# A new order of the pieces of a hand-scheduled transformer block, with equal tile modes of TensorE side by side

## The chip, the core and the metric

The kernel runs on one core of a Trainium2 chip. A core has five engines with a queue each: PE (TensorE, the matrix engine, whose weight loads are shown apart as PEld), DVE (VectorE), ACT (ScalarE), POOL (GpSimd) and SP (SyncE, which here only issues DMAs). Each engine works through its own instructions in order and waits on semaphores for the others. The metric is the device time of one execution in microseconds (us). Before the change the median of three runs was 3693.19 us (3692.50 to 3694.23).

## The reference

The computation is one block of a transformer with adaptive layer norm, for 8 sequences of 512 tokens with 128 features each.

```python
h = layernorm(x) * (1 + ca) + sa
x = x + ga * attention(h)          # 16 heads of 64, causal over all 512 tokens, softmax
h = layernorm(x) * (1 + cb) + sb
x = x + gb * local_layers(h)       # six layers, see below

for i in range(6):                 # local_layers
    x = attn_layer(shift_tokens(x), ...) + x
    x = ffn_layer(shift_tokens(x), ...) + x
```

`attn_layer` makes q, k and v of 16 heads, divides q and k by their norms, scales and rotates them by position, and lets each window of 32 tokens attend to itself and to the window before it. `ffn_layer` is a layer norm, a product to 2 x 341 features, one half times the GELU of the other, and a product back to 128. `shift_tokens` takes the second half of the features from the token before. All is float32.

## The kernel before

The work has two parts. The first is the global attention, in which the weights of the local layers are prepared beside it. The second is the six local layers. Each part is a set of software pipelines. A stage is a Python generator that emits a small piece of work, on one engine as a rule, and yields. `streams_of` gives each stage a letter and chains its pieces over all items in order. `run` then walks through a string of letters and emits the next piece of the stage that each letter names:

```python
with tc.manual_schedule():
    for s in order:
        next(streams[s])
```

So the string is the order in which every engine's queue is filled. `ORDER1` (5442 letters) is the string of the first part and `ORDER` (15688 letters) that of the second. Nothing reorders instructions later, and semaphores are set where a buffer or a value asks for one.

In the second part an item is a tile of 128 tokens. There are 4 tiles in a sequence, 8 sequences and 6 layers, so 192 tiles, and every stage below runs once for each tile (the number of pieces is in brackets):

- PE: `c` project (4: q and k, a 128x512 product in three matmuls each, lines L380 to L382), `j` turn_qk (4: four 128x128 transposes each, L937), `l` score (2, L981), `r` values (4: 128x512 products), `v` turn_p (2: four transposes each, L1080), `x` combine (2, L1106).
- ACT: `a` operand, `d` square (4, L856), `k` keep_qk (4: two pieces copy the turned keys into kbd by two half copies each, L946; two copy the turned queries, L950), `z` mask (2, L958), `o` exps (2, L1014), `s` keep_values (4, L1053), `w` keep_p (2, L1089), `y` keep_y (L1121).
- DVE: `e` rotate (4, L865), `g` square_sum (4, L892), `m` top (2, L995), `n` less_top (2, L1002), `p` denominator (4, L1022 and L1025). `h` inverse goes over DVE, ACT and POOL for two tiles at a time.
- POOL: `b` operand_rest, `f` rotate_sum (4, L883), `i` scale (2, L925), `q` divide (2, L1033).
- SP: `t` store (4, L1062) and `u` fetch (4, L1068), which write the values to DRAM and read them back in another layout for combine.

The letters `F` to `N` are the feed-forward layer of a sequence, with `F` its PE pieces (transposes L375, products, and L1149), `G` its ACT pieces (L1167 among them), `H` POOL and `I` DVE.

A matmul uses the PE array in a tile mode, given by how many rows and columns of the array it takes. Products and transposes use all of it, 128*128. Scores and combine work window by window, on 32 columns each, so they run in the mode 128*32, four windows side by side. In the first part the mixing of the values (L649) runs in 128*64 and the folding of weights (L745) on 64 rows.

The buffers that tie the stages together are few. PSUM has four banks for products, in turn (`psum_mm`: project, values, combine and the feed-forward layer share them), two for transposes (`psum_tr`) and one for each of the two halves of the scores (`sp0`, `sp1`). A PE piece that writes a bank waits until the engine that empties it is done.

```python
turn = {"mm": itertools.cycle(range(4)), "tr": itertools.cycle(range(2))}
```

In the first part the scores have two PSUM banks (`ss0`, `ss1`), products and transposes two each.

Of the kernel before, what the change touches and what calls it, by code (L numbers as in the profile page):

```python
# [27 lines left out]
    "aabaabcbcdcecefzargsfdecbedfrgfesdgcfgdcettbrcezdfsrgtfesdagcfgdrecscgdfettrbcesfduhucfehhhtgfedhhrgfrgsdhdgri"  # L28
    "sgtcasrdijejkcgcfdjkecbikejslkgdlfmdgjfejkrinckmrerzfajuuttuutsnjschfkghklethhzhsmlhobndfdmrzghocinscpzrdgiojp"
    "ptdjerkqekcfjpgsrkgjqaoelkftuuuutspldmfvppvwmcqwpncdqgzuxtesuidxnvyveocfwrgwtogfjsjekxipxkhcufdppujhyhhtcezqkj"  # L30
    "rpekqdlsglhmdfvnvhmwfrzgtruwnhscbgaiocezxoestfxdpjdfujygkrppickgcersqpjttedjkqrkgldufuagslmstfvnvwmcbzubncwieo"
    "rzxeofdxtspdfujgyFkppqcIrditjseckcefjtjkphrqkgrhuesufhhvdvgwtrsgfFadlIhhlIwbmhIcinmxzestrInxdfIuuojycoigkctptj"
    "serkjippckjezqlkpdguqlsumdgftvndvwrmfzeFsriGncwgrGeuajfotjsxgdfkhcHgckejtbxhkehhutslfyoFFdmdhpfGuppuhpGjrqnFFg"
    "GqgtcsIkvhidrwevsrawgbczfjzeltsikxmdxnfuugoFtjIjitykcrekicosjpdrefkuruzsrppftdjgslpaqglkmqFnmbvzvIuwcwntcsueoj"
    "zjefdrkcgftFFestdkhgfhFohhdprhIrhshriastjppckgcqdpcedqjjestlfglkfmxeikxmvnduvuygwfrznFwgbcsIojxkeFlIItutuioizd"
    "xfpuucyIjmdIrppqIkrstlasbpnrqmzveFwGvunfcGgzceHwctseujofxdkgxfedrtygoftcsgjpjddhrppkqreuhckuhhpajgsqFFtkeshGhG"
    "gvfvcflewldhmfwtFFgdniGmczuuIFdnijteorrIfsjgscgkbcerkjtiecdfjktgrdfkejarssgilohdxtsfzxphmhlhkupphuqrnyFpsmhqzF"
    "FIuuttnbhgoFizvIvowciwjejkcpfrkejdcsppdfckterqrseajfjpglgfdtlsmdgqxknxbmzgjkuicnutryuekiuoFtvsIlwfcmveFwrIIduf"
    "jduxsnkxoIgIpyIczrzdlstppqaFmjGpbnrqukejrGgjfkcgtchHesvhkchfvhuewdjwtglstfeoxkhmohxfdpdFFnuyzhuippGltpGgFFmqnG"
    "rqgzuoIvijcrwescstvfderwFagsfucdIkrebticstgojjedrkfcpdFppfkjsIjqktrpezcqasgjledflkmtfnxmzixgkFFnuuygdbohgjutho"  # L40
    "FhhukpvhIvhzwhriwcspprtdpqcesjdjqgkcevfdrwgrfseltsiaglkmxnfmxzntvbyuocuwFeorxsIfdjcpkjgrekFslIIuuttiizdxIfmcyp"
    "pjIdprnuqIkrzulsqsteaFbvmGfcnwvuGejwcHkgrefjdtjscgkfugrekjdlkhgtfhsxmhhtzxnohhdhlzigyuFFomupGtppGicjeFFkqpncGq"
    "IdujejzfckgFfekrdvsIfvwgtcwujidelogximxkndlogfzcpymrdpprqseartsbjtspjnfkFgcIqkjeFFukuofdtvgvowpFwhpprhqhhcIsrd"
    "hjhpsehrtqakcgsfuurzecbrdfetsvtvwgicdcwerfgjdjagdlfselkitmxmkxnfgjzuncusbtiyjkeuroukFslfIxmFnjIIozidlztktpxImr"
    "IyppcsqIrdrpesuqFuacGnfvtsevGcbwgrHweuojdjfckgxgfketsxudhlofghyphhFFdzmhhGpppGthrqtcnqgjrezivsFFukudGgfvtwlIus"
    "iwrmcnsajdbckertjdgfjseFkcIfukreoctitjgleskxfzmdxndfglzugyuoirtmcpsjndrkppqceFsajdpfIjoeFFktqgkvfvuugzwhFwbhro"
    "IthhrshchtsphcidpprdejrqkpescaqjgjstcgfdlgdfelkxmitekxvnfyuvumwrzgfjuuwncstbkFteiorzlIsfxmFnxIIodizjycpkrIgdIl"
    "uppuqIsrtcpseqaFdjmGufrekcbvnGfvwectsHjwecokjfugrgkfjedtlstkgfxzmdxhdnhloguhhzupryhmhFFthsppiGpGunFFgqrIGjqsjk"
    "ritcsvkecrwefajdvsgFftudtwcgkbxIoieljzmfjonckpixzdelkuuppjfrmdpjqynstckgrqecksgvfdvewFawFFbgdfIuozhFoghcphhrIh"
    "hdjhckeldtisppluqmxpefxnqjymjzrgfknckgiceFtsrtoefvdrwIrdfacsgubjuevkctsgFwfcejlIIuodzfdkplIppImqIpnFqstmuGveix"  # L50
    "zGvnwxgwHogtjtdjfocgykrpixesukxhufppjhdtcpuhhkgjqdrykerqszcgshFFfeaGrhGfvvbdlhwtgisuFFmwnGliIzjmFkncIocejjerfd"
    "cogdfceztFstkefFFkIfgjupFkupplqtddIuxxmlgynrgzrmscpsntiiquajdvoberwckgfretscstvhoefjdchwgfrhjuhkexusphhkfxtppd"
    "udlgqzgjymFhkrpnqrIzvsltisuawvmbFwinrIIrostjtIocIkrpIxadbxppsuqjuyejkctpgfrsekjrqkdcfuzgvdvwcewtiFsuleGfGlgdmH"
    "cmstjtndfcgkxnizexduoFFeuyfoGtprfpprGugjqjpsgFFsqhaGrbkItFscIhreckjfhhuezrtstvklfwdldmhhgvhsuinruwmcztgscuiand"
    "jdrekjbcefkjrgfkcetsujoirezklogdlfpdtmxstfppxnqcypmzrgqsujnuavdgbckitersvewFfwFFogdIfuogzFpstjhpphqjhhukcIrkhj"
    "hdphcqktetsxdiglelfmxmvnfyFutgzurIiwrsvsnFacwIIubocdIjoIerdkcIfxexstjyefzjukrpcfkgjeFdilktGgtlppsqdmGjpmfjkrnu"
    "rgqzuncktHgcaevsivsrewdrwgcfdhojjfuzetxhshhukgxfkolydphlbsmhtthFFppinGpGcmqrgdurznuqsejavstickgFFewfGvIdrwfgco"
    "FebtrsIjfdjuukcgicektrsteojfcdkpldfezximlsppxnqctpymzurugqejdvsfFwnaFFIktfgogbvuudFhwghocIhhzjjdhhtrkphirescst"
    "ppjkqrdgkrpeqxsagflstlfmxnimzjuynvukctbcewvoFzeuuicwfdrIdjsfrkejxsgfkFglIIttdoixpjIyppcIuurmdqIkrtslspnaqFezvb"
    "GcmfwvueGjwcHktgreufjdjsnckfgxektxtdgoflygohrzphdFFmuhhsuppGhhtpGcqnjerqFFzgfdGvgkrhIwivaslustwcuimcndjedrbkje"  # L60
    "fFsjkIcfttgrkeoicjglesfxztmkxfondpluziugdrppyrsmqjtspnrakqgcvesbcwvoefrdwjgsFfkhjFFIuuthkhhtdFohghzhpciIcdtrdi"
    "jesrkjesrafjtppscqgcpelqgldfmkxmfkexjbnyudfvugkrznvuuitwgctsFoerwiocIjrfeFalIIkzbfdjdplkImIuxppuqIsxstrypmqFnc"
    "GgvzvunGcewHcwojetfjsdgxkfuexdgkfrtgyotlhsphdFFmhhzppGhhupuGcqnreqjtFFzgfdGvgkrhIiwvasluswcimtjundckerbjdgfjse"
    "FkcIfttkreojicglesoxfkmtzxpdfnlduppyuzqrmcspnirteocsFgaqoejdvfkFFIpwfgvuutzppjbdrqwgkFphqgjhIschhktcdhvhdehvwi"
    "rwejscktfgrgdjfcsejdligtelkxfmmkxnfjgzujuniykrukuFascIobrresFsjIItitofcdlzpdIgIlmppxqIkxuucypeqtFdjGnrfkmrejGc"
    "znHvkecwfavsgjwtlgdfuesuxkbomxfdhortyzpFFhsnhhGpplhhpGtgqrmcqgzuFFnduhseiGtvovuIcgfrewcwijsejdrkgtFfrdIsfjugsc"
    "kicertktaejocfskpjdlfedzxmbflkpptxnqpmzjuygcquknriedvvoFgwwgFFfdIshogtjhuzpFhhukpprqIcshajhdtrbkpehrqsctgsfvdv"
    "wceiwrdgcsefrdtjgslfaelkimxgtnxfmzryunubFsuijIorkcjseFkxIIuttiozfldpxImIcppyqrIdjrkpueqsFulaGnftsgcGmbzujgHvdc"
    "nkerwcdgfvoetjsrwekfrjugoxfhktsxzplhypphhtdjqmFFkpnqsuguGlhthGchmivndvFFzuewiGgjwrIkfctujsejakcbfredFksgrftdtI"
    "jocgicersoeliskxptzmfxdppdlyuqnurpmzqtcgsnavdfvgwFwebjockIfreojjsprfuutktgFFppsqdhpkFgqhzchhIvhvhdwhcetiwcdgce"  # L70
    "djfjklgfedlkimxejxfnkmjuzfgrukunjysrgktiFourIscasbjeFlIIoizdflkpIxmtIppxqrItycsnrdpumzFquresGvtcnsfGvugwreHzca"
    "wgjfdcekjbretfsujkxgdfohlkoglhdpthhxtsmhppFFhyqnGpquGcmgFFuezhiGtvnvducIwwfjgdckeirjdgrsekfFtjgscfIakreobulixm"
    "sxnofzpczippyjdjdtprgtkecqslkeqcmfdvgvwFnwfFFeooIfdrprgusuppjaqjkgctuphbFehqsjhhkIkfldzvghlhmwhnvmrzwncxoestii"
    "cuofdrpdcgzppxdqstejtyjkerfrkpgfFgcuasIujqcktscbeFlefxIIuddfcmjIeItrxesfyIukfltgitFndvGgrgzivGmcshwdHnjhwcehho"
    "xukheuhfcotgjzfjupkxehkjppdflkgdplqymdgFFqnGrGmnFFzsGtigiFIuorIFFsFIabFrtIrsoctsjpdjkpprqcekjrefkjausrpguqkcst"
    "lfuzedlbmdfvmvwgrwncnzvtisveuiwxwgdxofgorhtystjphjhhkppcqcpekjqcuesujfkxdtkugfldezvhvhmwfldgwnxhmzrtigyuFnsria"
    "IorsjrkbtFtcIIsjoxdIpIkexursuIyfcatsrdppbjqejkckpglfuzelqmdtFgsufrnGcmizgcGdnrtseHvtdvwceofjwcogfkjeuxuispxtde"
    "krfppjuysrgakfjpgzlhkqdlmhstqughhFFnGhhGmrbnchzitvdtvsFFewiwgGrIojucfuretscsajfderkFgbfrdIkjugcktijesuloikpxdm"
    "zxppqstlntycpfgzmrdqnrevsujuawcbgoftvseFkcIfrdeojwFFpdfkgpptjqusFgukphzcqIhrhhdchesthjthdvikgcwevdrwfgjgrfecsa"
    "jdblstfelkimxmknxfgtjzunruykiFocsIrjesFlIIitukuotfzxdplImIppxqIcyjdpnrqkeFcGmvfzvnGruewuHcsajgwfrkejbdgjfkgcst"  # L80
    "huldehoxhhkmfoxgzpcdhnyhlhstppiudFFzgpeGGqFFmtqgtFGnrfIorIirsucausjeobctsrkeufFdpjfdjIkFFppqkgzFptgisucIcdqrde"
    "cistvevtwcwgfrgdrdgfjsejaklbestflkmxfmxngzvtnyvuwurhwujhsjuhhkchrhtekhtjiscorkeolfzpdjmfdlkppxqmpxnqgzcunyisuv"
    "eovtcwgwrfdeForspfuajdIxkbxppqstjygFkcpIIuizldgIrqettjscImrdnfIkrzliuasueFstjmfGucgkrnbveGcwHvezcdjfwgtrsgkjfu"
    "exdxhkfghdlthhsgtFFyhomhhoniGpppuuGcjrqejFFztipkdlsIGqugrkmvfncswvecatwbrzeuidjsjgkFfcIkjdfttelkolgimxmdxnfogr"
# [1237 lines left out]
```

## Time and profile before

| | |
|---|---|
| median of three runs | 3693.19 us |
| the profiled execution | 3693.09 us, its span 3691.3 us |
| PE busy | 97% of the span |
| DVE, ACT, POOL busy | 88%, 81%, 78% |
| first part (global attention) | up to about 860 us |
| second part (six local layers) | from there to the end |
| granted PE clock | 0.991 |

The profile is of one execution. "Busy" is the share of the span in which an engine has an instruction under way, so instructions that overlap in the engine's pipeline are counted once. Rows of waits name the waiting engine, its tile and line, who ended the wait, the sum in us, how often, and the longest. Rows of the timeline give the start, the length, the engine, line and operation, what it writes and reads, the tile mode (rows*columns of the array) for PE, the shape and how many like it follow each other. Matmuls are pipelined: the length of one is its way through the array, and what it costs the next is the distance of their starts.

### The profile page before, as it was taken

The page shows a single profiled execution, that of the slowest core. Times are in us where ns is not written, and L with a number is a line of the kernel's source. Part 1 is how long each engine was busy: PE and PEld are TensorE (multiplying, and loading weights), DVE is VectorE, ACT ScalarE, POOL GpSimd, SP SyncE. Part 2 cuts the span into 40 slices and gives each one's busy share as a digit, 9 for nine tenths or more (in the row PEclk, how much of TensorE's full clock was granted, in tenths as well). Part 3 has the DMA queues.
Part 4 walks back from the last instruction along what each step waited for, and adds up shares of the span by engine and source line. Part 5 has one row for each costly group of instructions (what it writes and reads, how often), then busy time and mean ns, then how long its engine had stood idle before and what let it go on. Part 6 is the DMA issues. An engine that isn't in the chain of part 4 may idle for free. (4 is left out here: it accounts for less than half of the span.)

```text
span 3691.3 us, 106123 instructions
## 1 busy us (share of the span) xinstructions
PE 3572.9 (97%) x40364; PEld 2776.9 (75%) x40364; DVE 3242.5 (88%) x6198; ACT 2977.8 (81%) x6342; POOL 2895.4 (78%) x3232
## 2 busy tenths in 40 slices
PE   7999999998999999999999999999999999999998
PEld 4566656665788878888788788888878887788786
DVE  5788988898999889999898889999898898989895
ACT  4666766676888888888888888988989888888886
POOL 3555556557998888898898888889888898888884
PEclk8999999999999999999999999999999999999999
DMA  7777778763554666546656557555666555666554
GB/s 193 199 188 191 180 193 177 179 148 101 146 145 135 164 179 166 155 134 166 179 154 163 137 158 183 155 159 137 168 179 163 150 143 147 184 161 160 154 161 110
DMA packets 352245, 594.75 MB, mean 161 GB/s; under 512 B 57198, under 2 KB 87532, under 8 KB 351740
## 3 DMA queue, kind: packets, MB, share of 16 engines
q1 hardware_dynamic: 349772, 585.70, 60.0%
q8 instruction: 323, 5.29, 0.6%
q10 hardware_dynamic: 1616, 2.16, 0.2%
q14 instruction: 182, 1.49, 0.1%
q0 software_dynamic: 352, 0.10, 0.1%
HBM read 254.52 MB, written 232.61 MB: 132 GB/s over the span
## 5 line engine op out<-in xcount | busy, mean ns | idle before, releaser
L883 POOL TENSOR_TENSOR rq<-u 128x512 f32<-128x512 f32 x768 | 983.2, 1292 | 144.9 <-DVE u L865 136.3
L865 DVE TENSOR_TENSOR u<-ps_mm,tab 128x1024 f32<-128x1024 f32 x768 | 926.3, 1218 | 127.6 <-PE ps_mm L382 63.6
L925 POOL TENSOR_TENSOR rq<-rq,rs_o 128x1024 f32<-128x1024 f32 x384 | 729.3, 1908 | 6.2
L621 POOL TENSOR_TENSOR pr<-pr,rd 128x512 f32<-128x512 f32 (+3 forms) x512 | 357.9, 721 | 297.7 <-DVE rd L614 279.2
L892 DVE TENSOR_REDUCE ss<-sq 128x8 f32<-128x512 f32 x768 | 511.5, 675 | 46.0 <-ACT sq L856 44.0
L856 ACT ACTIVATE sq<-ps_mm 128x512 f32<-128x512 f32 x768 | 458.9, 607 | 85.7 <-PE ps_mm L382 36.1
L1053 ACT COPY vh<-ps_mm 128x512 f32<-128x512 f32 x768 | 451.3, 593 | 80.7 <-PE ps_mm L382 56.9
L1033 POOL TENSOR_TENSOR pr<-pr,rd 128x256 f32<-128x256 f32 x768 | 457.1, 622 | 58.1 <-DVE rd L1025 44.5
L946 ACT COPY kbd<-ps_tr 64x512 f32<-64x512 f32 x768 | 446.3, 581 | 34.2 <-PE ps_tr L937 18.7
L937 PE MATMUL ps_tr<-ident,rq 128*128 128x128 f32 x3072 | 445.2, 274 | 4.2 <-DVE xs L1180 1.1
L937 PEld LDWEIGHTS ps_tr<-ident,rq 128*128 128x128 f32 x3072 | 363.3, 140 | 107.6 <-issue 25.9
L981 PE MATMUL sc<-kbd,qT 128*32 128x128 f32 (+1 forms) x13056 | 408.3, 266 | 7.5 <-issue 3.5
L602 ACT ACTIVATE pr<-ss,mx 128x512 f32<-128x512 f32 (+3 forms) x512 | 270.5, 529 | 176.5 <-DVE mx L592 155.9
L1106 PE MATMUL ps_mm<-v,pT 128*32 128x128 f32 x11904 | 401.8, 274 | 7.5 <-issue 7.3
L981 PEld LDWEIGHTS sc<-kbd,qT 128*32 128x32 f32 x13056 | 334.2, 109 | 69.8 <-issue 42.5
L1106 PEld LDWEIGHTS ps_mm<-v,pT 128*32 128x32 f32 x11904 | 341.4, 110 | 35.6 <-issue 24.9
L380 PE MATMUL ps_mm<-wvo,xa 128*128 128x512 f32 x768 | 347.0, 452 | 3.9 <-ACT sq L856 3.9
L380 PE MATMUL ps_mm<-wqk,xa 128*128 128x512 f32 x768 | 344.9, 449 | 5.7 <-ACT sq L856 4.0
L382 PE MATMUL ps_mm<-wqk,xa 128*128 128x512 f32 x768 | 304.8, 397 | 0.0
L382 PE MATMUL ps_mm<-wvo,xa 128*128 128x512 f32 x768 | 304.6, 397 | 0.0
L381 PE MATMUL ps_mm<-wvo,xa 128*128 128x512 f32 x768 | 303.0, 394 | 0.0
L381 PE MATMUL ps_mm<-wqk,xa 128*128 128x512 f32 x768 | 302.8, 394 | 0.0
(144 smaller groups left out, 8035.2 us busy)
## 6 DMA issues: line engine op xcount, KB each, us to landing
vd<-vh SPq DMA_DIRECT2D x768, 256.0 KB, 3.9
v<-vd SPq DMA_DIRECT2D x768, 256.0 KB, 5.1
both<-hi SPq DMA_DIRECT2D x384, 128.0 KB, 2.4
both<-lo SPq DMA_DIRECT2D x384, 128.0 KB, 2.4
wqk_d<-wqk SPq DMA_DIRECT2D x20, 512.0 KB, 3.4
wvo_d<-wvo SPq DMA_DIRECT2D x20, 512.0 KB, 3.8
wqk<-wqk_d SPq DMA_DIRECT2D x20, 512.0 KB, 4.1
wvo<-wvo_d SPq DMA_DIRECT2D x20, 512.0 KB, 4.8
```

The lines of the kernel that those rows point to most:

```text
L380: nc.tensor.matmul(ps, lhsT=xa[0], rhs=xb[0], start=start, stop=False)
L381: nc.tensor.matmul(ps, lhsT=xa[0], rhs=xb[1], start=False, stop=False)
L382: nc.tensor.matmul(ps, lhsT=xa[1], rhs=xb[0], start=False, stop=stop)
L856: nc.scalar.activation(sq, st["qk"][c], AF.Square)
L865: nc.vector.tensor_tensor(u, st["qk"][c].unsqueeze(1).to_broadcast([P, 2, 8, HD]), tabs[st["t"]][:, ts(c // 2, 2), :].unsqueeze(2).to_broa ...
L883: nc.gpsimd.tensor_tensor(r, a, b[:, :, ::-1, :], ALU.add)
L892: nc.vector.tensor_reduce(st["ss"][:, st["t"] % 2, ts(c, 8)], sq, AX.X, ALU.add)
L925: nc.gpsimd.tensor_tensor(rq, rq, rn[:, ts(side, 16)].unsqueeze(2).to_broadcast([P, 16, HD]), ALU.mult)
L937: nc.tensor.transpose(pt[:, ts(j, P)], flat[:, j, :], ident)
L981: nc.tensor.matmul(o[:, :, s], lhsT=q, rhs=kbd[:, :, j, k : k + n].rearrange("p e (s k) -> p e s k", k=WIN), start=False, stop=True, skip_ ...
L1033: nc.gpsimd.tensor_tensor(prg, prg, rd.unsqueeze(2).to_broadcast([P, 8, WIN]), ALU.mult)
L1106: nc.tensor.matmul(y[ts(w, WIN), :], lhsT=pT[:, s, g, ts(w, WIN)], rhs=vals, start=s == 1 and g == 0, stop=g == 3 and (s == 0 or (t == 0 a ...
```

## The change

Both strings are replaced. The pieces are the same, each letter appears as often as before, and the pieces of one stage keep their own order. What differs is how the stages are interleaved: pieces that use PE in the same tile mode stand next to each other more often. No function, buffer or shape changes.

```diff
 ORDER = (
-    "aabaabcbcdcecefzargsfdecbedfrgfesdgcfgdcettbrcezdfsrgtfesdagcfgdrecscgdfettrbcesfduhucfehhhtgfedhhrgfrgsdhdgri"
-    "sgtcasrdijejkcgcfdjkecbikejslkgdlfmdgjfejkrinckmrerzfajuuttuutsnjschfkghklethhzhsmlhobndfdmrzghocinscpzrdgiojp"
...
+    "aabaabcbcdcecefzargsfdecbedfrgfesdgcfgdrettbcsrgdftescargdbfescrgdfesccgdfettzrceusfudhcftehhhgfedhhrgfrgsdhdt"
+    "gcisgradceijdjgkcecfkjgbkejfslkdfelrmidmrncagfzuuttuutjesjrkinrkhfgjthsjhhzcbkhkehlshidldmsgconfojejzrikpcmkre"
...
 )
```

In the built program PE changes its tile mode 1097 times before and 857 times after: 445 and 397 times in the first part, 652 and 460 times in the second. In the second part the stretches of 128*32 work go from 326 to 230.

## The prediction

> **What bounds the kernel now.** I read the page first, then the busy time by stretch, then PE's own waits, then PE's instructions one by one.
>
> ```profile
> span 3691.3 us, 106123 instructions
> PE 3572.9 (97%) x40364; PEld 2776.9 (75%) x40364; DVE 3242.5 (88%) x6198; ACT 2977.8 (81%) x6342; POOL 2895.4 (78%) x3232
> ```
>
> The reader sees four engines that are all well used, with PE on top. By stretch (columns: PE, weight loads, DVE, ACT, POOL busy us, granted clock):
>
> ```profile
> 0.00:860.00 860.00, 795.24 (x4424) 526.50 (x4424) 712.83 (x2042) 557.22 (x1585) 458.29 (x642) 0.98 0.73 179
> 1500.00:2000.00 500.00, 497.94 (x6402) 404.27 (x6401) 452.64 (x742) 438.96 (x863) 438.76 (x472) 1.00 0.58 158
> 2000.00:2500.00 500.00, 497.60 (x6531) 404.36 (x6530) 450.63 (x747) 435.62 (x856) 438.62 (x465) 1.00 0.59 159
> 3600.00:3692.00 92.00, 75.00 (x949) 56.09 (x947) 53.78 (x102) 56.40 (x102) 41.80 (x44) 0.91 0.42 108
> ```
>
> The first part (global attention, up to about 860 us) has PE at 92%. The second part, the six local layers, has PE at 99.5% with a full clock, while DVE, ACT and POOL stand at 88 to 90%. So from 1000 to 3600 us the time is PE's own time. What PE waits for there:
>
> ```profile
> PE ps_mm L1106 <- issue: 7.3, 3, 4.0
> PE sc L981 <- issue: 3.5, 4, 1.4
> PE sc L981 <- ACT qT L950: 2.1, 4, 0.9
> ```
>
> These are the three largest rows between 1000 and 3600 us, small against 2600 us. "Issue" at L1106 is the combine step, which reads values that a DMA brought. Only a change of PE's own time, or many new waits, can move the end. PE's own time has a part that no row names, the change of tile mode. PE's timeline around 2100 us (start, length, instruction, count):
>
> ```profile
> 2099.92 0.39 PE L381 MATMUL ps_mm<-wqk,xa 128*128 128x512 f32 x1
> 2100.15 0.39 PE L382 MATMUL ps_mm<-wqk,xa 128*128 128x512 f32 x1
> 2100.38 0.60 PE L937 MATMUL ps_tr<-ident,rq 128*128 128x128 f32 x4
> 2100.91 0.75 PE L981 MATMUL sc<-kbd,qT 128*32 128x64 f32 x23
> ```
> ```profile
> 2103.49 1.12 PE L981 MATMUL sc<-kbd,qT 128*32 128x64 f32 x32
> 2104.54 0.51 PE L380 MATMUL ps_mm<-wvo,xa 128*128 128x512 f32 x1
> 2104.88 0.39 PE L381 MATMUL ps_mm<-wvo,xa 128*128 128x512 f32 x1
> 2105.11 0.39 PE L382 MATMUL ps_mm<-wvo,xa 128*128 128x512 f32 x1
> ...
> 2106.74 0.60 PE L937 MATMUL ps_tr<-ident,rq 128*128 128x128 f32 x4
> 2107.09 0.48 PE L380 MATMUL ps_mm<-wqk,xa 128*128 128x512 f32 x1
> 2107.41 0.39 PE L381 MATMUL ps_mm<-wqk,xa 128*128 128x512 f32 x1
> ```
>
> Between full-width products the starts are 0.23 us apart. Four transposes before a product take 2107.41 - 2106.74 = 0.67 us up to the second product, that is 4 x 0.109 and 0.233: no cost beyond their own. But four transposes before a 128*32 matmul take 0.53 us instead of 0.44, and the product after 128*32 work needs 0.34 us to its second matmul instead of 0.23, after a late first start. That is the price of a mode change.
>
> **The change part by part.** The letters of both order strings are the same set: 15688 and 5442 pieces, each letter as often as before. No engine computes anything more or less; the instruction order has 2617 DMA issues on SP, 10 on POOL and 5 on ACT, and 97 table loads, in both. So the working has four terms.
>
> *Term 1, mode changes of the local layers.* Counted in the instruction order, PE changes mode 652 times there before and 460 times after: 326 stretches of 128*32 become 230. The price, from the medians of all starts in this trace: transpose to 128*32 start 203 ns against 109 to the next transpose, product to 128*32 327 against 232, so 94 ns to go in. Coming out into a product, its second matmul starts 541 ns after the last narrow matmul; without a change it would be 233 for the product and 66 to 89 for the narrow one: 219 to 242 ns extra. Coming out into a transpose: 369 against 109 and the same 66 to 89, so 171 to 194 ns. The order loses 96 ways in, 60 ways out into products and 37 into transposes (and gains one into the feed-forward product): 96 x 0.094 + 60 x 0.219 + 37 x 0.171 = 28.4 us, with the other end 30.7 us. Nothing covers it: PE is at 99.5%. I take -28.4.
>
> *Term 2, the first part.* Mode changes there fall from 445 to 397, nearly all of them between 128*64 and full width, 24 stretches fewer. At the same 0.28 us for a pair (an estimate: 94 in, about 190 out) that is 6.7 us. But PE idles in 8% of this part, so part of it only becomes waiting. I counted in the order the places where PE waits for an engine that has itself just waited for PE, and where the PE work between (each instruction at its spacing in the trace) is less than the loop takes: matmul 397 ns, 36 ns to the copy's start, each copy queued ahead at its spacing (0.49 us of ACT for 128x512), the last one's 590 ns, 53 ns back to PE. What is missing in places that do not overlap sums to 60.9 us before and 64.5 after, +3.6. I take -6.7 + 3.6 = -3.1; ends -6.7 and +10, since the engines' loops set this part.
>
> *Term 3, waits of PE on ACT, DVE and POOL in the local layers.* Fewer and longer stretches mean that PE fills PSUM in longer bursts: 230 cycles in 2830 us are 12.3 us each, instead of 8.7. In the burst PE makes a 128x512 product every 0.70 us and four transposes every 0.44 us; ACT needs 0.49 us for a copy, and 1.2 us for the two kbd copies of each transposed K tile.
>
> ```profile
> 2103.35 1.10 ACT L856 ACTIVATE sq<-ps_mm 128x512 f32<-128x512 f32 x2
> ```
>
> Two copies in 1.10 us, so 0.49 apart and the second 0.60 long. The same count of short places gives 117 before (76 short by over 0.2 us) and 290 after (211). The typical new one is a score piece held back to join a narrow stretch: its qT copy (L950) stands behind a dozen other ACT instructions that the burst brought. Without overlap the shortage is 25.3 us before and 43.3 after. Before, PE really lost 34.1 us at 39 stalls where a short place stands, from the ends of consecutive PE groups less their spacing, 1.35 times what the count says. So after, 1.35 x 43.3 = 58.4, and the term is +24.3. The low end is 0 (a short place that the drift between engines absorbs), the high end scales by the number of places, 34.1 x 290/117 - 34.1 = +50. I take +24.3 because it is the only one tied to a measured stall. Who is late next: DVE and POOL wait behind the same bursts, but at 88 to 90% they catch up in the narrow stretches.
>
> ACT's share there is 439 of 500 us, against PE's 498. The Trainium skill (TensorEngine Tiling (Array Packing), section PSUM Bottleneck) says that tiling speeds up TensorE but not the emptying of PSUM, which may then be the limit, and wants ScalarE and VectorE to share it; this speaks against packing full-width pieces together. If it held outright, PE would save nothing and the time would stay near 3693; by the shares above it holds for single bursts only.
>
> *Term 4, DMA.* Store and fetch of the values (L1062, L1068) land in 3.9 and 5.1 us. The order now puts the combine step later behind its fetch: waits on a fetch with under 6 us of PE work between fall from 45 to 24 of 758. The L1106 row above, 7.3 us, shrinks in this proportion: -3.4. Ends -7.3 and 0.
>
> Sum: -28.4 - 3.1 + 24.3 - 3.4 = -10.6. The profiled execution took 3693.09 us (span 3691.3 and 1.8 around it), the median of the runs is 3693.19. 3693.1 - 10.6 = 3682.5, which I round to 3683. A measurement of this kernel tells about 0.2% (7.4 us) from no change.
>
> **The rivals.**
>
> *A, the whole gain arrives.* The short places are absorbed, as most are now (117 places, 39 stalls): -28.4 - 6.7 - 3.4 gives 3655. For it: ACT, DVE and POOL have 10% to spare. Against it: the short places are not just more, 211 instead of 76 are over 0.2 us.
>
> *B, nothing to be measured.* The gain is real and the new waits take all but 7 us of it: waits of +28 to +42 in term 3, 3686 to 3700. For it: the two terms are of one size.
>
> *C, slower: ACT's bursts become the bound.* The place is the score and product pieces behind L950, L946, L856. If stalls grow with the number of short places the term is +50, and the sum -28.4 - 3.1 + 50 - 3.4 = +15, 3708. It decides from about +42 us in term 3. For it: PE has no cover left to hide a late copy. Against it: it needs a larger growth than the shortage itself shows.
>
> That the change does not do what it says is no rival: the counts of mode changes are read from the built order. A mode change removed where PE waits anyway is worth nothing, though; that is term 2's upper end.
>
> **How the numbers follow.** The forecast's case, faster by 7 to 25 us: 0.40. A, 25 us or more: 0.15. B: 0.21. C: 0.24. The likeliest is the forecast, 3683, its own range 3668 to 3686. For 8 in 10 I reach down into A (3655) and up through B into C (3708): 3656 to 3708. Faster 0.40 + 0.15 = 0.55, same 0.21, slower 0.24.
>
> **What would show it.** Term 1: PE's 128*32 stretches fall by a third, with the same 94 ns in and 220 out, and PE's busy time falls. If the starts after a mode change cost less in longer stretches, it is wrong. Term 3: the rows of PE and of the weight loads waiting for ACT L950, L946, L856 and L1053 grow by about 24 us in the local layers, and the waits of ACT for PE grow too. If they stay, A is right; if they double, C. Term 4: the issue row of L1106 shrinks. Term 2: the first part ends within a few us of 860.

## The result and the profile after

| | median us | runs | against before, 95% interval |
|---|---|---|---|
| before | 3693.49 | 6 (3690.12 to 3696.70) | |
| after | 3712.48 | 6 (3706.22 to 3717.53) | 1.0051 (1.0038 to 1.0064) |

The new order is 19 us slower, 0.5%. The forecast was 3683 with a range of 3656 to 3708, so the sign was wrong, and the time lies above the range. Rival C (3708, slower) came nearest. The profiled execution of after took 3713.16 us, with a span of 3711.4, against 3693.09 and 3691.3 before.

The page of after, the lines that answer to those of before (busy us, share, instructions of each engine):

```profile
span 3711.4 us, 106154 instructions
PE 3567.7 (96%) x40364; PEld 2793.0 (75%) x40364; DVE 3229.6 (87%) x6198; ACT 2972.2 (80%) x6342; POOL 2895.0 (78%) x3232
```

PE has the same 40364 instructions and is busy for 5 us less, in a span that is 20 us longer. By stretch (PE, weight loads, DVE, ACT, POOL busy us, then granted clock):

```profile
0.00:860.00 860.00, 791.53 (x4427) 530.11 (x4427) 713.07 (x2054) 554.65 (x1585) 461.97 (x643) 0.99 0.73 179
1500.00:2000.00 500.00, 495.88 (x6454) 405.86 (x6456) 451.36 (x741) 436.73 (x863) 440.26 (x472) 1.00 0.58 157
2000.00:2500.00 500.00, 491.58 (x6459) 403.09 (x6448) 446.96 (x743) 431.51 (x849) 432.22 (x462) 1.00 0.58 158
```

In the layers PE fell from 497.9 and 497.6 of 500 us to 495.9 and 491.6. Nobody else took over: from 1000 to 3600 us DVE, ACT and POOL are each a little less busy than before. The same columns, first before, then after:

```profile
1000.00:3600.00 2600.00, 2576.86 (x33543) 2096.51 (x33542) 2349.41 (x3871) 2256.82 (x4441) 2272.72 (x2422) 1.00 0.58 159
1000.00:3600.00 2600.00, 2552.09 (x33178) 2088.63 (x33169) 2319.86 (x3822) 2229.42 (x4395) 2247.11 (x2395) 0.99 0.58 157
```

So no engine became the bound over the whole stage, and what was lost shows first in gaps of PE. PE's own waits between 1000 and 3600 us, after (who waits, for whom, us in total, times, longest):

```profile
PE ps_mm L1106 <- issue: 9.1, 3, 3.2
PE ps_mm L380 <- issue: 7.7, 5, 3.7
PE sc L981 <- issue: 5.7, 3, 3.8
PE ps_tr L937 <- ACT kbd L946: 3.5, 5, 1.3
PE ps_tr L937 <- POOL rq L925: 3.3, 2, 2.5
PE sc L981 <- ACT sc L958: 2.0, 2, 1.7
```

Three of these rows before, which the prediction does not show:

```profile
PE ps_tr L375 <- issue: 1.8, 1, 1.8
PE ps_tr L937 <- ACT kbd L946: 0.7, 1, 0.7
PE ps_tr L937 <- POOL rq L925: 0.6, 1, 0.6
```

All rows of this view add up to 21.9 us before and 45.1 after. Two kinds grew most: those that ACT ends (4.4 to 13.9 us) and those with "issue", where no semaphore is behind the wait (12.6 to 23.2). Those that POOL ends went from 2.1 to 5.5. The growth of the "issue" rows is no accident of one execution: in the five profiles with the old order of the layers (before and four of the experiments below) they add up to 9.8 to 15.9 us, in the five with the new one to 21.0 to 26.0. These rows hold only time in which PE has nothing under way at all. To have the rest I took, for each group of PE instructions in the layers (a product, four transposes, a stretch of narrow work), the time from the end of the group before to its own end, and subtracted its instructions' own spacing and the mode change. What is left over is the group's stall. So "own work" in this table is a count times spacings, not a time read off the trace:

| layers, us | before | after | difference |
|---|---|---|---|
| PE from the end of the first part to its last instruction | 2830.4 | 2854.7 | +24.3 |
| its own work, mode changes included | 2762.0 | 2733.2 | -28.8 |
| stalls | 68.4 | 121.5 | +53.1 |

The stalls of over 0.15 us (119 of them with 67.8 us before, 222 with 124.5 after) by what ended them:

| stall ended by | before | after |
|---|---|---|
| ACT | 22.6 | 50.6 |
| DVE | 15.2 | 16.6 |
| POOL | 2.4 | 8.7 |
| the fetch of the values (L1068) | 13.2 | 19.0 |
| no semaphore | 14.4 | 29.0 |

0.6 us of after stand in none of these rows.

The first part's last matmul ends at 851.6 us, 4.2 earlier than the 855.8 of before.

### The profile page after: what moved, and what is told of

It is laid out like the page before. It is cut to its first block, busy times and chain, and to the rows that moved or that the text cites. A ratio compares the mean times of both kernels' runs of the same rounds, so it can differ in the third digit from the quotient of the medians.

```text
span 3711.4 us, 106154 instructions
## 1 busy us (share of the span) xinstructions
PE 3567.7 (96%) x40364; PEld 2793.0 (75%) x40364; DVE 3229.6 (87%) x6198; ACT 2972.2 (80%) x6342; POOL 2895.0 (78%) x3232
## 3 DMA queue, kind: packets, MB, share of 16 engines
q8 instruction: 323, 5.29, 0.6%
q14 instruction: 182, 1.49, 0.1%
## 5 line engine op out<-in xcount | busy, mean ns | idle before, releaser
L883 POOL TENSOR_TENSOR rq<-u 128x512 f32<-128x512 f32 x768 | 983.6, 1292 | 132.3 <-DVE u L865 124.5
L925 POOL TENSOR_TENSOR rq<-rq,rs_o 128x1024 f32<-128x1024 f32 x384 | 728.6, 1908 | 5.8
L937 PE MATMUL ps_tr<-ident,rq 128*128 128x128 f32 x3072 | 449.6, 276 | 14.4 <-ACT kbd L946 3.7
L1106 PE MATMUL ps_mm<-v,pT 128*32 128x128 f32 x11904 | 399.7, 273 | 12.4 <-issue 9.1
L1106 PEld LDWEIGHTS ps_mm<-v,pT 128*32 128x32 f32 x11904 | 348.9, 110 | 17.8 <-issue 9.5
L382 PE MATMUL ps_mm<-wqk,xa 128*128 128x512 f32 x768 | 305.4, 398 | 0.0
L382 PE MATMUL ps_mm<-wvo,xa 128*128 128x512 f32 x768 | 304.9, 397 | 0.0
L381 PE MATMUL ps_mm<-wqk,xa 128*128 128x512 f32 x768 | 304.1, 396 | 0.0
L381 PE MATMUL ps_mm<-wvo,xa 128*128 128x512 f32 x768 | 303.0, 394 | 0.1
```

Of the source, the lines that this page charges most:

```text
L381: nc.tensor.matmul(ps, lhsT=xa[0], rhs=xb[1], start=False, stop=False)
L382: nc.tensor.matmul(ps, lhsT=xa[1], rhs=xb[0], start=False, stop=stop)
L883: nc.gpsimd.tensor_tensor(r, a, b[:, :, ::-1, :], ALU.add)
L925: nc.gpsimd.tensor_tensor(rq, rq, rn[:, ts(side, 16)].unsqueeze(2).to_broadcast([P, 16, HD]), ALU.mult)
L937: nc.tensor.transpose(pt[:, ts(j, P)], flat[:, j, :], ident)
L1106: nc.tensor.matmul(y[ts(w, WIN), :], lhsT=pT[:, s, g, ts(w, WIN)], rhs=vals, start=s == 1 and g == 0, stop=g == 3 and (s == 0 or (t == 0 a ...
```

## The experiments

**The two strings apart.** The first two kernels each take one new string and leave the other:

```diff
 e1_first_part_new:  ORDER of before,  ORDER1 of after
 e2_layers_new:      ORDER of after,   ORDER1 of before
```

> The new ORDER1 (first part) with the old ORDER (layers). In the two traces the first part ends at 855.8 us before and 851.6 us after. Theory (all of the loss is made in the layers): about 4 us under the kernel before, 3689, at most 8 under it. Rival (the loss begins in the first part, or the layers start worse from its end): 3693 or more.

> The old ORDER1 with the new ORDER (layers). Theory: the layers took 2830 us of PE's time before and 2855 after, so 3693 + 24 = 3717, between 3710 and 3724. Rival (the two parts only lose together): less than 8 us above the kernel before.

Measured: e1 3689.97 us against 3695.9 for before on the same chip, ratio 0.9984 (0.9975 to 0.9993). e2 3716.03, ratio 1.0054 (1.0041 to 1.0066). The first stretch of e1:

```profile
0.00:860.00 860.00, 791.88 (x4426) 531.15 (x4426) 712.62 (x2053) 555.11 (x1585) 462.05 (x643) 0.98 0.73 179
```

PE's busy time there is that of after (791.5), and its instruction count is within one of it. So the first part's string gains its few us, and the whole loss sits in the layers' string. By the ratios e1 is faster than both kernels, by 0.16% and 0.67%.

**ACT made lighter.** The key copies and the exponentials are halved, in both orders. The part left out is named in the expectations.

```diff
-                nc.scalar.copy(kbd[r, e, ts(n, 4), pos : pos + P], st["pt"][n][r])
+                nc.scalar.copy(
+                    kbd[r, e, ts(n, 4), pos : pos + HD], st["pt"][n][r][:, :, :HD]
+                )
...
-            prg = st["pr"][:, :, ts(g, 8), :]
+            prg = st["pr"][:, :, ts(g, 8), : WIN // 2]
```

> Both old orders, with work taken from ACT: the copies of the turned keys take 64 of 128 positions (64x256 instead of 64x512, 768 times), and the exponentials of the layers half of the columns (384 times); kbd is zeroed whole at the start. The result is not the reference's. Theory (PE waits for ACT after bursts): PE stalls that ACT ends are 22.6 us in the layers before, so 5 to 20 us faster than the kernel before, 3673 to 3688. Rival (PE's extra waits come from DMA and instruction supply): 3690 to 3694.

> The same work taken from ACT (half of the key copies, half of the exponentials, so another result) under both new orders. Theory (ACT behind in bursts is what ate the 28 us): the stalls that ACT ends were 50.6 us, most go, and the saved mode changes show: at or under the old orders with the same light ACT, by 0 to 20 us. Rival (DMA, instruction supply, or mode changes that were never dear): it stays 15 to 22 us above them.

Measured: old order 3682.07, ratio 0.9957 (0.9945 to 0.9970); new order 3681.03, ratio 0.9952 (0.9939 to 0.9966). The gap between the orders goes from +19 to -1 us; each ratio is known to about 0.13%, 5 us, so it is closed to within some 7 us. The transposes of the keys and queries between 860 and 3700 us, first in after, then in e4 (line, operation, count, busy us and mean ns, idle us ahead of them and what ended it):

```profile
L937 PE MATMUL ps_tr<-ident,rq 128*128 128x128 f32 x3072 | 449.6, 276 | 14.4 <-ACT kbd L946 3.7 <-POOL rq L925 3.3 <-ACT pT L1089 1.7
```
```profile
L937 PE MATMUL ps_tr<-ident,rq 128*128 128x128 f32 x3072 | 445.8, 275 | 9.5 <-POOL rq L925 4.7 <-ACT qT L952 2.3 <-ACT kbd L946 0.7
```

The wait behind the key copies falls from 3.7 to 0.7 us. POOL's does not (3.3 and 4.7). Over the layers the stalls that ACT ends are 50.6 us in after and 26.0 in e4 (16.0 in e3), and all stalls are 92.3 in e4 and 63.8 in e3, a difference of 28.5 where after and before differ by 53.1. So about 25 of the 53 us hung on ACT's load, and without them the 28.8 us of PE's own work pay for the other 28.5. The edit takes work from ACT everywhere, so it does not tell ACT's bursts from its load as a whole. What is left in e4 against e3 is stalls without a semaphore (27.5 against 16.5), POOL (10.9 against 2.9) and ACT (26.0 against 16.0).

**The price of a mode change.** Ahead of each of the 768 products of the values stands one more matmul, which the product overwrites; once on 32 columns, which forces a change in and out, once on all 128:

```diff
+            nc.tensor.matmul(
+                ps[:WIN, :HD], lhsT=ident[:, :WIN], rhs=ident[:, :HD], start=True, stop=True
+            )
```
```diff
+            nc.tensor.matmul(
+                ps[:P, :HD], lhsT=ident[:, :P], rhs=ident[:, :HD], start=True, stop=True
+            )
```

> The kernel before, with one small extra matmul before each of the 768 values products, in the mode 128*32 (32 stationary columns, 64 moving), into the bank that the product then overwrites. It is the price of a mode excursion by itself. Theory (an excursion costs 0.28 us of PE and nothing covers it): 768 pieces, some 10% of them already beside narrow work, so 690 x 0.28 + 768 x about 0.06 = 240 us above the kernel before, at least 170. Rival (a mode change hides behind the waits of other engines, or costs little): under 100 us.

> The same 768 extra matmuls with all 128 stationary columns, so without a change of mode. Theory: only their own time, about 768 x 0.06 to 0.12 = 45 to 90 us above the kernel before, and the difference to the narrow ones is the price of 690 pairs of changes, 130 to 210 us. Rival (an extra matmul costs as much in either mode): the two are within 40 us.

Measured: e5 3970.91, ratio 1.0747 (1.0730 to 1.0764), +275 us; e6 3849.64, ratio 1.0415 (1.0398 to 1.0433), +154 us. PE's timeline in e5 (start, length, line, operation, mode, count):

```profile
2100.21 0.39 PE L381 MATMUL ps_mm<-wvo,xa 128*128 128x512 f32 x1
2100.44 0.40 PE L382 MATMUL ps_mm<-wvo,xa 128*128 128x512 f32 x1
2100.77 0.30 PE L1043 MATMUL ps_mm<-ident 128*32 128x64 f32 x2
2101.00 0.50 PE L380 MATMUL ps_mm<-wvo,xa 128*128 128x512 f32 x1
2101.34 0.39 PE L381 MATMUL ps_mm<-wvo,xa 128*128 128x512 f32 x1
```

The narrow matmul starts 0.33 us after the product's last, where 0.23 is the spacing within a product, and the next product's second matmul 0.34 us after its first instead of 0.23. From L382 to the next L381 there are 0.90 us here and 0.46 without the dummy. That is +0.44 for a pair of changes and the dummy's own time; over the whole run, 275 us by 768 is 0.36 each. The full-width dummy missed its expectation: I took 45 to 90 us for it and it cost 154. In its trace the distance from L382 to the next L381 has a median of 0.69 us, so the dummy adds 0.22 to the 0.46. The difference of the two runs, 121 us, also missed its 130 to 210. e5 has 2481 mode changes and e6 1097, so it is 0.175 us for each of 692 pairs, if both dummies cost the same. The two runs put a pair's price between that and the 0.36 us that still have the narrow dummy in them. The 0.28 of the prediction lies between, and nothing here narrows it further. That a change costs PE time that nothing covers is shown; its size in the new order rests on the spacings: the median way in is 327 ns behind a product and 203 behind a transpose in both traces.

**The DMA load.** The new order moves stores and fetches of the values. To see whether the semaphore-less stalls come from this traffic, half of the stores are left out:

```diff
-        st["vd"] = l3d.tile([P, 4, 512], F32, tag="vd", name="vd")
+        if st["t"] % 2:
+            st["vd"] = st["prev"]["vd"]
+        else:
+            st["vd"] = l3d.tile([P, 4, 512], F32, tag="vd", name="vd")
         for h in range(4):
-            nc.sync.dma_start(st["vd"][:, h], st["vh"][h])
+            if st["t"] % 2 == 0:
+                nc.sync.dma_start(st["vd"][:, h], st["vh"][h])
```

> Both old orders; the values are stored to DRAM for every second tile only (384 stores of 256 KB instead of 768), and the odd tiles fetch what the tile before stored, so the result is not the reference's. Theory (part of PE's stalls are full DMA engines: late values, and late instructions for PE, the stalls that no semaphore ends): the old order has 13 and 14 us of such stalls in the layers, so 5 to 15 us faster than the kernel before, 3680 to 3691. Rival (those stalls are not of the DMA load): 3693 to 3697.

> The same half of the stores left out (another result) under both new orders, which have 20 us of stalls on fetched values and 29 us that no semaphore ends. Theory: these fall most here, and the distance to the old orders with the same stores shrinks from 19 us to 4 to 12. Rival: it stays at 17 to 22.

Measured: old order 3700.53, ratio 1.0015 (1.0006 to 1.0024); new order 3716.37, ratio 1.0054 (1.0041 to 1.0067). Neither gained, and the gap is 16 us, between the 4 to 12 of the theory and the 17 to 22 of its rival. Stalls without a semaphore are 14.6 and 29.6 us, the same as with all stores. The theory that the traffic of the stores causes them falls. The load of the fetches was not reduced, so this run says nothing on them.

**ACT and DMA lighter together** (both edits above):

> Both old orders with both reliefs: half of the key copies and of the exponentials off ACT, and every second tile's stores left out (the result is not the reference's). Theory: 3666 to 3678, the two reliefs add.

> Both new orders with both reliefs (another result too). Theory (28 us of mode changes are saved and were eaten by ACT's bursts and by DMA): under the old orders with the same reliefs by 8 to 25 us. Rival (the saving is smaller than counted, or a third cause eats it): within 5 us of them.

Measured: 3686.00, ratio 0.9973 (0.9963 to 0.9984), and 3685.50, ratio 0.9979 (0.9970 to 0.9988). The gap is about 0 again, not the -8 to -25 that the theory of two causes asked for, and the old order missed its 3666 to 3678 as well. Lighter stores add nothing, with ACT lighter too: stalls without a semaphore stay at 15.6 and 27.9 us. So something other than the stores makes them.

**The supply of instructions.** What the semaphore-less stalls have in common is what stands ahead of them. After, around 3480 us (start, length, line, operation, mode, count, and in brackets the idle time and what ended it):

```profile
3476.33 0.61 PE L375 MATMUL ps_tr<-ident,xs 128*128 128x128 f32 x4
3476.86 2.01 PE L981 MATMUL sc<-kbd,qT 128*32 128x64 f32 x80
3478.67 1.95 PE L1106 MATMUL ps_mm<-v,pT 128*32 128x128 f32 x56
3480.55 0.66 PE L937 MATMUL ps_tr<-ident,rq 128*128 128x128 f32 x4
3484.94 0.59 PE L380 MATMUL ps_mm<-wvo,xa 128*128 128x512 f32 x1 [3.73 <-issue]
```

A stretch of 136 narrow matmuls, each with its weight load, is 272 instructions in 3.7 us. After it, PE does four transposes, and then nothing for 3.73 us, though no semaphore holds it. The page of before has a queue that it calls "instruction":

```profile
q8 instruction: 323, 5.29, 0.6%
```

323 packets and 5.29 MB are 16.4 KB a packet, and PE's 2 x 40364 matmuls and weight loads by 323 are 250 to a packet. In after, each of the ten "issue" gaps of over 0.4 us between 1000 and 3600 us ends 1.16 to 1.56 us after such a packet has landed, and in before each of the seven, 1.21 to 1.49 us after one. That is a coincidence of times so far. To test it I put more narrow instructions into combine that cost PE little and ask nothing of any other engine:

```diff
         y = st["yp"] = psum_mm()[:, :D]
+        for n in range(32):
+            nc.tensor.matmul(
+                y[ts(n % 4, WIN), :8],
+                lhsT=pT[:, 1, 0, ts(n % 4, WIN)],
+                rhs=v[:, n % 4, 0, :8],
+                start=True,
+                stop=True,
+                skip_group_check=True,
+            )
         for s in (1, 0):
```

> Old order; ahead of combine 32 more 128*32 matmuls of 8 columns for every tile, which the next one overwrites: 12288 more PE and weight-load instructions in the narrow stretches, with little array time each, and no more work for ACT, DVE, POOL or the DMA of values. Theory 'instruction supply' (blocks of 256 PE instructions come no closer than about 3.5 us, so PE runs dry after long stretches of quick narrow instructions): the stalls of PE with no semaphore behind them in the local layers, 14.5 us before, grow to 35 us or more, each ending 1.2 to 1.7 us after an instruction block has landed, while the stalls that ACT ends (22.6) shrink, since PE becomes slower. Rival 'these stalls have to do with mode changes or with the fetched values': the number of mode changes and the fetches stay the same, so they stay at 12 to 18 us. The time grows by the matmuls' own cost, an estimate of 8 to 28 ns each, 50 to 170 us, and does not tell the theories apart.

> New order with the same 32 additional narrow matmuls of 8 columns for every tile. Theory 'instruction supply': from 29.0 us the stalls with no semaphore grow to 60 us or more, by more than in the old order, since the narrow stretches are longer; the gap to the old order with the same matmuls is 25 us or more, against 19 without them. Rival: 26 to 32 us, and the gap is 19 or less, as PE, now slower, waits less for ACT.

Measured, in two runs of each: old order 3989.86, ratio 1.0786 (1.0754 to 1.0817); new order 4012.95, ratio 1.0848 (1.0795 to 1.0901). The old order took 292 us more than before, where I had expected 50 to 170. PE's waits between 1000 and 3600 us in e11, where the matmuls above are L1096 and combine's own are L1115:

```profile
PE ps_mm L1115 <- issue: 74.9, 40, 5.3
PE sc L981 <- issue: 23.0, 15, 3.6
PE ps_mm L1096 <- issue: 16.7, 7, 5.2
```

and of the page of e11:

```profile
PE 3742.4 (94%) x52652; PEld 2928.0 (73%) x52652; DVE 3244.5 (81%) x6198; ACT 2989.7 (75%) x6342; POOL 2896.2 (73%) x3232
q8 instruction: 419, 6.86, 0.8%
```

Each of the 6144 matmuls became two PE instructions with a weight load each, 24576 instructions, twice what my expectation had counted. The queue has 96 packets more: exactly 256 instructions to a packet, so it is PE's program that this queue brings. The "issue" waits went from 12.6 us in 8 gaps to 120.8 in 68, and of 56 such gaps of over 0.4 us in that window 55 end 1.12 to 1.61 us after a packet has landed. The fetches of the values and the work of the other engines were left as they were, so those are ruled out as the cause of the growth. The number of mode changes is the same too (1097). The theory holds for the old order. The rows that ACT ends were to shrink there and did not: 4.4 us before, 4.7 in e11. For the new one the growth is as large (23.2 to 130.6 us in 83 gaps), not larger, and the gap between the orders is 23 us, between the 25 that the theory asked for and the 19 of its rival. With two runs of each (3987 and 3992, 4005 and 4021) that gap tells neither from the other. It may be that the order hardly matters for the supply once every stretch is dense; no run shows it.

## Why the prediction was wrong

*Term 1, mode changes of the local layers (-28.4): right, as far as it can be seen.* By counts and spacings PE's own work fell by 28.8 us (the term's own sum, with its prices as printed, gives 28.5). The ways in cost the same in the new trace: the timeline above has the same 0.53 us from the transposes of L375 to a narrow stretch as before the change.

*Term 2, the first part (-3.1): right in size.* The last matmul of the first part ends 4.2 us earlier, and e1 gains 5.9 us with an interval of 2.6 to 9.2. Its two parts, mode changes and waits, were not measured apart.

*Term 3, waits on ACT, DVE and POOL (+24.3): the count was right and the term too narrow.* At the counted short places the stalls went from 34.1 us (39 stalls) to 60.9 (101), where the forecast had 58.4; those of them that ACT, DVE or POOL end are 33.6 and 58.9, +25.3. But stalls that these three engines end at places that I had not counted went from 6.6 to 17.0, +10.4 more. The count looked only at places where PE's consumer loop itself is short of cover. An ACT that works through a burst also comes late to places that have enough cover by themselves. That is the forecast's sentence "DVE and POOL wait behind the same bursts, but at 88 to 90% they catch up in the narrow stretches", and it failed: the POOL stalls went from 2.4 to 8.7 us. With the term at 25.3 + 10.4 = +35.7 the sum would have been +1, no change.

*Term 4, DMA (-3.4): the step that was wrong in kind.* I read "L1106 <- issue" as a wait for fetched values and let it shrink in the proportion of short fetches. The row is, in the trace of before too, a PE that has run out of instructions. Its longest wait there stands in the middle of one combine piece, behind 131 narrow matmuls:

```profile
3110.61 2.01 PE L981 MATMUL sc<-kbd,qT 128*32 128x64 f32 x80
3112.43 1.83 PE L1106 MATMUL ps_mm<-v,pT 128*32 128x128 f32 x51
3118.24 0.46 PE L1106 MATMUL ps_mm<-v,pT 128*32 128x128 f32 x5 [3.99 <-issue]
```

It did not shrink, it grew from 7.3 to 9.1 us, and all "issue" rows from 12.6 to 23.2. With what PE loses around them, stalls without a semaphore are +14.6 us, and those at the fetch of the values +5.8. Part of this is a term that the sum does not have at all: it takes the full clock for granted, and behind the new gaps the clock falls (last section), which is worth up to 11 us by an estimate there. The new order does to this cause the reverse of what I assumed: it joins narrow stretches, and long narrow stretches are what empties the supply. Together +20.4 where -3.4 stood, this is the larger of the two errors (24 us against 11).

*The sum.* Measured terms: -28.8 of own work and -4.2 in the first part; +35.7 at ACT, DVE and POOL, +20.4 without a semaphore and at the fetches, and -3.0 in what is left, the stalls of under 0.15 us above all. That is +20.1, the difference of the two spans. Rival A fails by the first table. Rival B was the outcome that term 3 alone would have brought. Rival C had the sign and, with 3708, nearly the time, and e3 and e4 show its cause at work: with lighter ACT the loss is gone within some 7 us. But its mechanism, a term 3 of +50, was reached by 70% only. The rest is a cause that none of my rivals had, so C came near in part by luck.

The Trainium skill's rule that I weighed (TensorEngine Tiling (Array Packing), section PSUM Bottleneck: tiling speeds up TensorE but not the emptying of PSUM) fits more of what happened than I gave it. I took it to hold for single bursts only and the time to be safe since ACT had 12% to spare. e3 and e4 show that some 25 us hung on ACT all the same. That it was single bursts fits ACT's busy time, 2229 of 2600 us, but no run here shows it apart from the load.

What stays open is how the rest of the growth at POOL and DVE would behave alone, which no run separates, and what sets the moment at which a packet of instructions is asked for.

## What to carry to other kernels

Grouping work of one tile mode saves a real price for each change, but it made two other rhythms coarser here: the engine that empties PSUM gets its work in bursts, and PE uses up its instructions in bursts. With PE at 99%, an average share of 88% for the next engine did not mean that it was always in time, so cost a reordering by the longest burst it makes as well as by totals. A wait that the profile calls "issue" is to be looked into before it is put down to a DMA of data: see how many instructions ran just before it and whether a packet of the instruction queue landed shortly ahead of its end.

## What the hardware showed that I had not expected

*PE can run dry of instructions.* In the layers of after, packets of 256 instructions landed every 9.6 us in the median and never closer than 3.58 us, which is 72 instructions in a us; in e12, the hungriest kernel, never closer than 3.25. The narrow stretch shown above used 272 in 3.69 us, 74 in a us, so it runs near the fastest supply that any of these traces has, and it is longer than a packet. The mean from 1000 to 3600 us of after is 102 instructions in 4 us; all but two of its ten gaps came behind some 200 to 270 in 4 us. The gap of 3.73 us above has its packet in this stretch of the DMA view:

```profile
q1 hardware_dynamic: 242, 0.44, 101.0%
q8 instruction: 1, 0.02, 5.6%
```

These are the queues between 3482.4 and 3483.6 us of after. The data queue takes the whole of the engines' time there. Whether that delays the packet of instructions is not shown: halving the stores left these stalls as they were, and the fetches were not reduced.

*A gap is paid twice.* After the 3.73 us the granted clock is down for several us. Windows of after (length, then PE, weight loads, DVE, ACT, POOL busy and the clock):

```profile
3481.40:3485.00 3.60, 0.06 (x1) 0.06 (x1) 2.23 (x6) 1.01 (x2) 2.38 (x4) 0.75 1.05 300
3485.00:3487.00 2.00, 2.00 (x8) 1.62 (x7) 0.00 (x0) 0.58 (x2) 0.00 (x0) 0.50 0.32 62
3487.00:3489.00 2.00, 2.00 (x9) 1.61 (x8) 0.45 (x1) 0.79 (x3) 0.41 (x1) 0.50 0.40 142
3489.00:3491.00 2.00, 2.00 (x11) 1.67 (x10) 1.31 (x2) 1.59 (x3) 1.14 (x1) 0.74 0.00 0
3491.00:3493.00 2.00, 2.00 (x14) 1.58 (x12) 2.00 (x4) 2.00 (x5) 1.31 (x2) 1.00 0.00 0
```

The clock is at 0.50 for 4 us and back at 1.00 after 6, and the products' matmuls start 0.43 us apart meanwhile instead of 0.23:

```profile
3485.32 0.63 PE L381 MATMUL ps_mm<-wvo,xa 128*128 128x512 f32 x1
3485.75 0.63 PE L382 MATMUL ps_mm<-wvo,xa 128*128 128x512 f32 x1
```

Before has one gap as long (3.99 us, ending at 3118.24) and the same drop after it, to 0.62 and 0.53 in the two windows of 2 us that follow. Between 1000 and 3600 us that is its only one; after has six. Each stretch at half the clock, first the one of before, then those of after, in the same columns:

```profile
3118.48:3121.89 3.41, 3.41 (x15) 2.79 (x11) 0.11 (x1) 2.81 (x6) 0.46 (x1) 0.50 0.00 0
```
```profile
1254.31:1261.14 6.83, 5.51 (x17) 4.05 (x18) 2.42 (x3) 2.34 (x4) 2.36 (x3) 0.50 0.10 31
2186.15:2189.56 3.41, 3.41 (x27) 2.79 (x28) 0.42 (x1) 1.25 (x3) 0.00 (x0) 0.50 0.02 7
2711.80:2715.21 3.41, 3.06 (x12) 2.67 (x13) 1.21 (x3) 2.35 (x5) 3.39 (x3) 0.50 1.00 261
3148.70:3155.53 6.83, 5.75 (x28) 3.74 (x28) 1.04 (x3) 3.45 (x8) 1.88 (x2) 0.50 0.50 127
3363.74:3367.15 3.41, 3.41 (x11) 2.72 (x12) 1.23 (x1) 0.85 (x2) 0.00 (x0) 0.50 0.68 154
3483.21:3490.04 6.83, 5.10 (x17) 4.12 (x17) 1.64 (x2) 2.00 (x4) 1.73 (x4) 0.50 0.49 124
```

PE is busy for 26.2 us in them, against 3.4 before. If all of that work ran at half speed, the clock cost 13.1 us against 1.7, an estimate of up to 11 us of the loss; the table of stalls does not show it apart. Five of the six gaps ahead of them are "issue" waits (2.93, 2.96, 3.21, 3.73 and 3.81 us), one is a wait for POOL at L925 (2.51 us). The Trainium skill (TensorE: Matmul & The Clock Gate, Part 1: The HAM clock gate) says that an idle window of about 3.4 us puts the array to half its clock. The lengths of the stretches, 3.41 us or twice that, fit such a window, but four of these gaps were shorter than 3.4 us and the clock fell all the same, while two gaps of 3.1 us in e11 left it at 1.00.
